# Two network layers on eight images: seven assisted taps and shift sums on ScalarE in image 0, an unfolded layernorm in image 1, large banks for the last gelus

## The chip, the cores and the metric

The kernel runs on one core of a Trainium2 chip. The metric is the device time of one execution in microseconds (us), the median of several runs. Engines are named PE (TensorE, the matrix engine), DVE (VectorE), ACT (ScalarE), POOL (GpSimd, which here issues DMAs only) and SP (SyncE, also DMAs only). Each engine takes its instructions in the order in which they were written for it; across engines, semaphores set the order.

## The reference, cut to what matters

The input is eight images of 384 channels on 32 x 32 points, all in float32. Layer 0 is a transformer block on the 1,024 points, layer 1 a convolution block:

```python
xn = layernorm(xf, g1, beta1)                       # first layernorm  (ln1)
q, k, v = split(xn @ w_qkv.T + b_qkv)               # 8 heads of 48
out = softmax(q @ k.T * SCALE) @ v
x1 = out @ w_proj.T + b_proj + shortcut
xn2 = layernorm(x1, g2, beta2)                      # second layernorm (ln2)
h = gelu(xn2 @ w_fc1.T + b_fc1)                     # 1536 wide
x = x1 + h @ w_fc2.T + b_fc2

y = conv_7x7_depthwise(x, dw_w) + dw_b
y = layernorm(y) * ln_w + ln_b                      # third layernorm  (ln3)
y = gelu(y @ w1 + b1)
gx = sqrt(sum over points of y*y);  nx = gx / (mean(gx) + eps)
y = grn_gamma * (y * nx) + grn_beta + y
return x + y @ w2 + b2
```

## The kernel before, in words

**Tiles.** Channels lie on the 128 partitions: an image is CT = 3 channel tiles of N = 1024 points, handled in halves of NH = 512. The hidden layer has HT = 12 tiles. The PSUM accumulators come from two pools: two large banks of 1024 columns (tag `s`, made by `s_tile`, used for attention's scores, for every second product of fc2 and for some sums) and four small ones of 512 columns (tag `o`, made by `o_tile`). A tile whose pool is exhausted waits until the last reader of the oldest one is done. A matmul of 128x512 in float32 is two records in the trace and takes U = 0.857 us.

**Order of the work.** The program is straight-line code. The matmuls are written out by hand, and each advances a planned clock (`flow.pe(us)`) of the class `Flow`. Work of the other engines is written as generators that are handed to `flow.spawn`; a generator emits its next instructions when the planned clock passes the wait that it yielded last. `flow.finish(chain)` emits all that a generator has left at once, at that place of every queue. So the planned waits decide where an instruction stands in its engine's queue, and nothing else; when it runs is up to the chip.

**Stages.** For image b the program writes: q and k, attention, the first half of fc1 (twelve tiles `fc1_b_0_m`, each followed by a gelu on ACT, L457 through `other_table`), the second half, fc2, and then layer 1 of image b-1: the w1 products (`grn_up`, whose matmuls are `h_*`), the values of the next image, and the w2 products. The depthwise convolution of image b-1 runs beside image b.

**The convolution.** It has 49 taps for each channel tile. DVE does most of them (`convolution`, L1102, about 1.15 us each). The generator `help_convolution` takes the last `helped` taps of each channel tile: ACT multiplies half an image by the tap (L1123, 128x512) into one of four buffers, and POOL issues a DMA of 256 KB that adds the result to the accumulator (L1124). HELPED is 7; image 0 has `HELPED + 2` (L1668). When fc1's first half of image b ends, `end_soon` finishes both generators, waits a planned time, and then the third layernorm of image b-1 runs (`conv_norm`).

**The third layernorm.** `abreast` runs two `layernorm` generators, one for each half. The sum over the channels is a matmul with a matrix of ones (`token_sums`). With a fold, a DMA by POOL first adds one half of the partitions to the other, and two 64-row matmuls that fill one after the other of the partition halves do the rest at half the price; with `fold=None` it is one 128x512 matmul of full price without a DMA. The first layernorm of image b+1 (`norm_of_next`) runs at about the same time and keeps its folds; its sums use the large banks, its variances the small ones. For these two norms DVE subtracts the mean (L1740 and L513), ACT squares, DVE adds the squares, and the variances go through ln and exp on ACT.

**fc2.** `by_thirds` forms fc2 of images 0 to 6 out of fifteen products of four matmuls, p0 to p14, alternately in a small and a large bank; DVE makes their operands and adds the products to `x` (L954 and L957). At the end `pad_half` copies `x` into the padded image with ACT (L891).

**Image 0's attention.** There the DVE also prepares weights, among them two shifts: the bias of w1 gets the layernorm's shift times w1 added (`shift_through_w1`), that of w2 the GRN's shift times w2 (`shift_through_w2`). Column sums on PE (L273, 128x1 each, into a large bank) give what is added; DVE adds the bias by L1501 (three columns at once, two groups for each of two steps) and L1519 (one column, three times). The scores of attention use the same large banks. The row sums of the softmax go through a chain for each pair of heads: ACT copies (L717), DVE adds (L719), a DMA carries out the row sums, DVE takes the reciprocal (L726), DMAs carry it back as `r`, and DVE multiplies (L745) before the projection.

**The last image.** `mlp_by_halves` does fc1 and fc2 one half of the points after the other. After fc2 of the first half, DVE adds (L895) and ACT pads (L891); twelve tiles of fc1's second half follow with their gelus. In the same stretch DVE does the last image's convolution and the third layernorm of image 6, whose sums lie in the large banks.

Of the kernel before, what the change touches and what calls it, by code (L numbers as in the profile page):

```python
# [46 lines left out]
F32 = mybir.dt.float32  # L47
# [4 lines left out]
P = 128  # L52
# [123 lines left out]
def block_kernel(  # L176
# [73 lines left out]
    def col(name, i):  # L250
        at, width = VEC[name]
        assert i < width
        return vec[:, at + i : at + i + 1]
# [7 lines left out]
    def o_tile(name):  # L261
        return ps_o.tile([P, NH], F32, tag="o", name=name)

    def weighted(dst, part, name, k):

        if k == 0:
            nc.vector.tensor_scalar(dst, part, col(name, 0), None, ALU.mult)
        else:
            nc.vector.scalar_tensor_tensor(dst, part, col(name, k), dst, ALU.mult, ALU.add)
# [6 lines left out]
    def columns(name):  # L276
        at, width = VEC[name]
        return vec[:, at : at + width]
# [93 lines left out]
            flow.pe(2 * U)  # L372
        return ps

    def linear_half(lhsT, rhs, nk, h, name):
        ps = o_tile(name)
        for k in range(nk):
            nc.tensor.matmul(out=ps, lhsT=lhsT(k), rhs=rhs(k)[:, half(h)], start=(k == 0), stop=(k == nk - 1))  # L378
            flow.pe(U)
        return ps  # L380
# [75 lines left out]
    def other_table(dst, src, function, **kw):  # L456
        nc.scalar.activation(dst, src, function, **kw)  # L457
        table[0] = None

    def s_tile(name):  # L460
        return ps_s.tile([P, N], F32, tag="s", name=name)

    def token_sums(t, name, fold, wait, bank):

# [408 lines left out]
                    nc.sync.dma_start(out=other, in_=own)  # L873
                proj("x", xt, qt * P // NH)

    def gelu_half(hid, m, h, xn, weights, wname, name):
        w = weights.at(wname, m // CM)[:, m % CM * CT : (m % CM + 1) * CT, :]
        ps = linear_half(lambda k: w[:, k, :], lambda k: xn[:, k, :], CT, h, f"{name}_{h}_{m}")
        other_table(hid[:, m, half(h)], ps, AF.Gelu, bias=bfc1[:, m : m + 1])

    def difference(dst, more, less):
# [150 lines left out]
    def mlp_by_halves(b, xt, xn, weights, ln, rest, between):  # L1032

        hid = one.tile([P, HT * N], F32, tag="big", name=f"hid_{b}").rearrange("p (m n) -> p m n", m=HT)
        for h in range(2):
            wa, wb = f"fc1_{b}_{h}", f"fc2_{b}_{h}"
            flow.finish(ln)
            for m in range(HT):
                gelu_half(hid, m, h, xn, weights, wa, f"fc1_{b}")
                if m % CM == CM - 1:  # L1040
                    weights.used(wa, m // CM)
                if m == 5 and h == 0:
                    rest()
                    ln = flow.spawn(layernorm(xt, xn, 1, eps0, "g2", f"ln2_{b}", True, slow=2.0))
                if m == HT - 1 and h == 0:
                    between(0, -1, ln)
            for ct in range(CT):
                keys = RAW[2 * ct : 2 * ct + 2]
                tiles = [weights.at(wb, key)[:, k, :] for key in keys for k in range(6)]
                ps = linear_half(lambda k: tiles[k], lambda k: hid[:, k, :], HT, h, f"fc2_{b}_{ct}_{h}")  # L1050
                for key in keys:
                    weights.used(wb, key)
                add_first(xt, ct, h, ps)
                pad_half(xt, ct, h)
                between(h, ct)
# [48 lines left out]
            n += 1  # L1104
            yield share * next((early for m, early in first if n <= m), us)

    def help_convolution(acc, us, taken, helped):

        yield 8.0
        for ct in reversed(range(CT)):  # L1110
            taken[ct] = float("inf")
            for i in TAPS[KS * KS - helped :]:
                dy, dx = divmod(i, KS)
                for h in range(2):
                    if quiet:
                        while quiet:
                            yield 1.0
                        yield 3.0
                    t = three.tile([P, NH], F32, tag="res", bufs=4, name=f"tap_{ct}_{i}_{h}")
                    y0 = dy + h * H // 2  # L1120
                    window = pad[:, ct, y0 : y0 + H // 2, dx : dx + W]
                    tap = col("dww", ct * KS * KS + i)
                    nc.scalar.mul(t.rearrange("p (h w) -> p h w", w=W), window, tap)  # L1123
                    nc.gpsimd.dma_start(out=acc[:, ct, half(h)], in_=t, accum_op=ALU.add)  # L1124
                    yield us
            taken[ct] = flow.now + 8.0
        yield 8.0
        taken.clear()
# [187 lines left out]
    def after(first, chain, us=0):  # L1316
        if us:
            yield us
        while first is not None and first.gi_frame is not None:
            yield 1.0  # L1320
        yield from chain
# [88 lines left out]
    def prepare(weights, aside):  # L1410
# [72 lines left out]
        def shift_through_w1():  # L1483
            for i in range(0, HT // 2, CT):
                t = one.tile([P, CT, N], F32, tag="xn", bufs=2, name=f"w1_lnb_{i}").rearrange("p c n -> p (c n)")
                t = t[:, : CT * 6 * P]
                nc.gpsimd.dma_start(out=t, in_=w1[:, i * 6 * P : (i + CT) * 6 * P])
                t = t.rearrange("p (i a o) -> p i a o", a=6, o=P)
                yield 22.0
                for r, order in enumerate(((0, 1, 2), (5, 3, 4))):  # L1490
                    dst = t[:, :, order[0], :]
                    nc.vector.tensor_scalar(dst, dst, col("lnb", 0), None, ALU.mult)
                    for k in (1, 2):
                        nc.vector.scalar_tensor_tensor(dst, t[:, :, order[k], :], col("lnb", k), dst, ALU.mult, ALU.add)
                yield 5.0
                ps = ps_s.tile([P, N], F32, tag="s", name=f"b1_{i}")
                for r, a in enumerate((0, 5)):
                    for k in range(CT):
                        column_sums(ps, r * CT + k, t[:, k, a, :])
                    m = i + r * HT // 2  # L1500
                    nc.vector.tensor_tensor(b1[:, m : m + CT], ps[:, r * CT : (r + 1) * CT], columns("b1")[:, m : m + CT], ALU.add)  # L1501

        def shift_through_w2():
            for r in range(CT):
                t = blocks(f"w2_gbeta_{r}")
                for s in range(2):
                    nc.gpsimd.dma_start(out=t[:, s], in_=chunk(w2, 2 * r + s).rearrange("p (k o) -> p k o", o=P))
                yield 14.0
                h = HT // 2
                for s in range(2):  # L1510
                    g = columns("gbeta")[:, s * h : (s + 1) * h].unsqueeze(2).to_broadcast((P, h, P))
                    nc.vector.tensor_tensor(t[:, s], t[:, s], g, ALU.mult)
                nc.vector.tensor_tensor(t[:, 0], t[:, 0], t[:, 1], ALU.add)
                for k in range(1, h):
                    nc.vector.tensor_tensor(t[:, 0, 0, :], t[:, 0, 0, :], t[:, 0, k, :], ALU.add)
                yield 8.0
                ps = ps_s.tile([P, N], F32, tag="s", name=f"b2_{r}")
                column_sums(ps, 0, t[:, 0, 0, :])
                nc.vector.tensor_tensor(b2[:, r : r + 1], ps[:, :1], col("b2", r), ALU.add)  # L1519

        if aside:
            yield from shift_through_w1()
# [92 lines left out]
    def main():  # L1615
# [49 lines left out]
        def start_conv(b, us, *first):  # L1665
            acc = state["acc"] = one.tile([P, CT, N], F32, tag="acc", name=f"acc_{b}")
            taken = {}
            helped = HELPED if b else HELPED + 2  # L1668
            state["conv"] = flow.spawn(convolution(acc, us, first, taken=taken, helped=helped), paced=True)
            state["help"] = flow.spawn(help_convolution(acc, 2.7, taken, helped), paced=True)  # L1670

        def conv_norm(b, ln):

            if b == 0:
                xn = state["xn"]
                norm = abreast(xn, xn, eps0, "g1", "ln1_1", True, gentle=True)
                state["norm1"] = flow.spawn(after(ln, norm))
            else:
                acc = state["acc"]
                how = dict(wait=5.0, late=3.5) if b < B - 1 else dict(factor=2.4, bank=s_tile)  # L1680
                norm = abreast(acc, acc, eps1, "lnw", f"ln3_{b - 1}", True, **how)
                if b < B - 1:
                    state["norm1"] = flow.spawn(after(ln, norm_of_next(b, 22.0 if b > 1 else 34.0)))
                    state["norm3"] = flow.spawn(after(ln, sequence(end_soon(b), norm)))
                else:
                    state["norm3"] = flow.spawn(after(ln, after(state["help"], after(state["conv"], norm))))
# [17 lines left out]

        def end_soon(b):
            end_convolution(b)
            yield 16.0 if b > 1 else 28.0

        def norm_of_next(b, us):

# [302 lines left out]
```

## Time and profile before

| quantity | value |
|---|---|
| median of 5 runs | 3269.34 us (3268.52 to 3273.7) |
| profiled execution | 3269.43 us, span 3267.7 us |
| granted TensorE clock, mean | 0.995 |
| PE busy | 3231.8 us (99%) |
| DVE busy | 2423.1 us (74%) |
| ACT busy | 1669.7 us (51%) |
| POOL busy | 486.9 us (15%) |

The busy time of an engine is the time in which it ran at least one instruction. A line of the timeline is a run of like instructions: its start and length in us, engine, source line, operation, output and inputs, shape, number, and in brackets the idle time of the engine ahead of it and what ended it. A line of the waits is engine, line, what it waited for, then the total in us, how often, and the longest. A line of the windows is start and end in us, length, then busy time with the number of instructions for PE, weight loads, DVE, ACT and POOL, the granted TensorE clock (1.00 is full), the mean busy share of the DMA engines and GB/s.

### The profile page before, as it was taken

What the parts mean: (1) busy time and instruction counts of PE and PEld (TensorE: products, weight loads), DVE (VectorE), ACT (ScalarE), POOL (GpSimd) and SP (SyncE); (2) the same over time, 40 slices, a digit from 0 to 9 for tenths busy, and PEclk for the clock granted to TensorE, in tenths of its full rate; (3) what the DMA queues carried; (4) which work ended last, traced back from release to release, by engine and by line L of the source; (5) the groups of instructions that cost most, each with busy time, mean ns of one, the idle gap of its engine ahead of it and who ended that gap; (6) DMA issues with size and microseconds to landing.
All of it is one profiled execution on the core that took longest, in us unless ns stands there. A gap on an engine that the chain in (4) does not pass through costs nothing. (4 is left out here: it accounts for less than half of the span.)

```text
span 3267.7 us, 38881 instructions
## 1 busy us (share of the span) xinstructions
PE 3231.8 (99%) x14204; PEld 1390.5 (43%) x14204; DVE 2423.1 (74%) x3309; ACT 1669.7 (51%) x2328; POOL 486.9 (15%) x575
## 2 busy tenths in 40 slices
PE   9999998999999999999999999999999999999999
PEld 5334433443344433444344443344434444344455
DVE  4544786778877878678787787876878778879940
ACT  3452664365743566434754537636475375723641
POOL 2111212102211121101212012110211102200000
PEclk9999999999999999999999999999999999999999
DMA  6535744638426473355734466353843638433231
GB/s 213 209 111 121 162 91 76 146 98 190 95 58 161 112 171 79 66 157 127 151 75 99 130 169 123 62 127 105 198 94 58 149 100 197 79 79 91 63 97 54
DMA packets 204114, 387.70 MB, mean 119 GB/s; under 512 B 41232, under 2 KB 46992, under 8 KB 203536
## 3 DMA queue, kind: packets, MB, share of 16 engines
q0 software_dynamic: 82880, 169.38, 27.6%
q1 hardware_dynamic: 120752, 215.09, 21.7%
q8 instruction: 114, 1.87, 0.2%
q10 hardware_dynamic: 288, 0.71, 0.1%
q14 instruction: 80, 0.66, 0.1%
HBM read 199.61 MB, written 38.14 MB: 73 GB/s over the span
## 5 line engine op out<-in xcount | busy, mean ns | idle before, releaser
L1102 DVE SCALAR_TENSOR_TENSOR acc<-pad,vec,acc 128x930 f32<-128x930 f32 (+8 forms) x855 | 956.2, 1154 | 29.1 <-DMA acc<-tap 24.3
L767 ACT ACTIVATE p<-s 128x1024 f32<-128x1024 f32 x512 | 524.4, 1025 | 275.3 <-PE s L758 268.9
L758 PE MATMUL s<-qk 48*64 48x512 f32 x4096 | 540.4, 594 | 6.1 <-DVE b_f L1519 5.6
L778 PE MATMUL o<-p,v 64*64 64x512 f32 x4096 | 537.0, 591 | 0.0
L378 PE MATMUL fc<-xn,fc 128*128 128x512 f32 x1152 | 506.2, 596 | 17.2 <-ACT hid L457 15.0
L1124 POOL DMA_DIRECT2D acc<-tap x306 | 263.9, 873 | 1449.3 <-ACT tap L1123 710.1
L378 PEld LDWEIGHTS fc<-xn,fc 128*128 128x128 f32 x1152 | 217.6, 190 | 301.6 <-issue 271.9
L445 PE MATMUL fc_p<-hid,fc 128*128 128x512 f32 x728 | 318.1, 593 | 1.1 <-DVE hid L957 0.6
L778 PEld LDWEIGHTS o<-p,v 64*64 64x64 f32 x4096 | 160.7, 133 | 282.9 <-issue 277.2
L758 PEld LDWEIGHTS s<-qk 48*64 48x64 f32 x4096 | 157.0, 133 | 289.2 <-issue 228.3
L457 ACT ACTIVATE hid<-fc,bfc_f 128x512 f32<-128x512 f32 x192 | 129.4, 684 | 286.8 <-PE fc L378 286.6
L445 PE MATMUL o_p<-y,w 128*128 128x512 f32 x624 | 270.9, 592 | 0.0
L1123 ACT ACTIVATE tap<-pad,vec 128x512 f32<-128x512 f32 x306 | 224.7, 735 | 19.0 <-DMA acc<-tap 19.0
L445 PEld LDWEIGHTS fc_p<-hid,fc 128*128 128x128 f32 x728 | 137.5, 190 | 178.4 <-issue 169.9
L445 PEld LDWEIGHTS o_p<-y,w 128*128 128x128 f32 x624 | 118.0, 190 | 148.7 <-issue 134.9
L1102 DVE SCALAR_TENSOR_TENSOR acc_last<-pad,vec,acc_last 128x377 f32<-128x377 f32 (+24 forms) x288 | 177.2, 688 | 0.6
L891 ACT COPY pad<-x 128x512 f32<-128x512 f32 x48 | 30.1, 634 | 254.4 <-DVE x L957 196.2
L719 DVE TENSOR_TENSOR attn<-o,attn 128x512 f32<-128x512 f32 x64 | 44.1, 689 | 131.3 <-ACT attn L717 131.3
L700 PE MATMUL proj<-attn,wproj_sb 128*128 128x512 f32 x288 | 127.2, 595 | 0.0
L678 PE MATMUL v<-wv_sb,xn 128*128 128x384 f32 x384 | 126.8, 487 | 0.0
L432 DVE TENSOR_TENSOR y<-h_n,y 128x512 f32<-128x512 f32 x72 | 49.8, 692 | 62.2 <-PE h_n L416 59.9
L678 PEld LDWEIGHTS v<-wv_sb,xn 128*128 128x128 f32 x384 | 72.5, 190 | 50.1 <-issue 3.4
(376 smaller groups left out, 4054.9 us busy)
## 6 DMA issues: line engine op xcount, KB each, us to landing
acc<-tap POOLq DMA_DIRECT2D x306, 256.0 KB, 3.5
fc<-s_fc SPq DMA_DIRECT2D x91, 256.0 KB, 4.0
w<-s_w SPq DMA_DIRECT2D x72, 320.0 KB, 3.5
hid<-hid POOLq DMA_DIRECT2D x42, 512.0 KB, 7.5
fc<-in_wfc SPq DMA_DIRECT2D x54, 384.0 KB, 4.1
w<-s_w SPq DMA_DIRECT2D x78, 256.0 KB, 2.7
y<-y POOLq DMA_DIRECT2D x36, 512.0 KB, 6.9
w_A<-in_w SPq DMA_DIRECT2D x36, 384.0 KB, 3.3
```

Of the source, the lines that this page charges most:

```text
L378: nc.tensor.matmul(out=ps, lhsT=lhsT(k), rhs=rhs(k)[:, half(h)], start=(k == 0), stop=(k == nk - 1))
L432: nc.vector.tensor_tensor(c[dst], banks(name), c[other], ALU.add)
L445: nc.tensor.matmul(out=bank, lhsT=lhsT, rhs=rhs, start=k == 0, stop=k == len(pairs) - 1)
L457: nc.scalar.activation(dst, src, function, **kw)
L678: nc.tensor.matmul(out=ps[:, :C], lhsT=xn[:, k, t * P : (t + 1) * P], rhs=wv_sb[:, k, :], start=(k == 0), stop=(k == CT - 1),)
L700: nc.tensor.matmul(out=ps, lhsT=wproj_sb[:, m, ct * P : (ct + 1) * P], rhs=attn[:, m, :], start=(m == 0), stop=(m == CT - 1),)
L758: nc.tensor.matmul(out=s[64 * i : 64 * i + 64, j, :], lhsT=kT[64 * j : 64 * j + HD, m, k0 : k0 + 64], rhs=qT[64 * j : 64 * j + HD, m, half ...
L767: nc.scalar.activation(p, s, AF.Exp)
L778: nc.tensor.matmul(out=outs[i][64 * j : 64 * j + 64, :], lhsT=v[keys, t, at : at + 64], rhs=p[keys, j, :], start=(t == 0), stop=(t == KT - 1),
L1102: nc.vector.scalar_tensor_tensor(dst, window, tap, dst, ALU.mult, ALU.add)
L1123: nc.scalar.mul(t.rearrange("p (h w) -> p h w", w=W), window, tap)
L1124: nc.gpsimd.dma_start(out=acc[:, ct, half(h)], in_=t, accum_op=ALU.add)
```

## The change

Four edits:

- Image 0 gets seven helped taps for each channel tile, as the others: twelve half taps fewer on ACT and POOL in all, six more taps on DVE.
- The fifteen shift sums of image 0 are read out of PSUM by ACT, one column an instruction (12 and 3 activations), in place of 4 and 3 adds on DVE.
- In image 1 the third layernorm of image 0 has no folds; its planned waits are stretched (`slow=1.6`), the wait ahead of it goes from 28 to 33, and that of the first layernorm of image 2 from 34 to 37.
- In the last image the gelus of fc1's second half read from the two large banks instead of the four small ones, and the sums of the third layernorm of image 6 lie in small banks.

The order of the other engines' instructions is the same from image 2 on; PE's own order differs only around the norms of image 1.

```diff
-    def linear_half(lhsT, rhs, nk, h, name):
-        ps = o_tile(name)
+    def linear_half(lhsT, rhs, nk, h, name, bank=o_tile):
+        ps = bank(name)[:, :NH]
...
-    def gelu_half(hid, m, h, xn, weights, wname, name):
+    def gelu_half(hid, m, h, xn, weights, wname, name, bank=o_tile):
...
-        ps = linear_half(lambda k: w[:, k, :], lambda k: xn[:, k, :], CT, h, f"{name}_{h}_{m}")
+        ps = linear_half(lambda k: w[:, k, :], lambda k: xn[:, k, :], CT, h, f"{name}_{h}_{m}", bank)
...
-                gelu_half(hid, m, h, xn, weights, wa, f"fc1_{b}")
+                gelu_half(hid, m, h, xn, weights, wa, f"fc1_{b}", s_tile if h else o_tile)
...
-            for i in TAPS[KS * KS - helped :]:
+            for i in TAPS[KS * KS - HELPED :]:
...
-                    nc.vector.tensor_tensor(b1[:, m : m + CT], ps[:, r * CT : (r + 1) * CT], columns("b1")[:, m : m + CT], ALU.add)
+                    for k in range(CT):
+                        bias = dict(bias=col("b1", m + k), scale=1.0)
+                        nc.scalar.activation(b1[:, m + k : m + k + 1], ps[:, r * CT + k : r * CT + k + 1], AF.Identity, **bias)
...
-                nc.vector.tensor_tensor(b2[:, r : r + 1], ps[:, :1], col("b2", r), ALU.add)
+                nc.scalar.activation(b2[:, r : r + 1], ps[:, :1], AF.Identity, bias=col("b2", r), scale=1.0)
...
-            helped = HELPED if b else HELPED + 2
-            state["conv"] = flow.spawn(convolution(acc, us, first, taken=taken, helped=helped), paced=True)
-            state["help"] = flow.spawn(help_convolution(acc, 2.7, taken, helped), paced=True)
+            state["conv"] = flow.spawn(convolution(acc, us, first, taken=taken, helped=HELPED), paced=True)
+            state["help"] = flow.spawn(help_convolution(acc, 2.7, taken), paced=True)
...
-                how = dict(wait=5.0, late=3.5) if b < B - 1 else dict(factor=2.4, bank=s_tile)
+                how = dict(wait=5.0, late=3.5, fold=b > 1, slow=1.0 if b > 1 else 1.6) if b < B - 1 else dict(factor=2.4)
...
-                    state["norm1"] = flow.spawn(after(ln, norm_of_next(b, 22.0 if b > 1 else 34.0)))
+                    state["norm1"] = flow.spawn(after(ln, norm_of_next(b, 22.0 if b > 1 else 37.0)))
...
-            yield 16.0 if b > 1 else 28.0
+            yield 16.0 if b > 1 else 33.0
```

## The prediction

> **What bounds the kernel now.** First the page's busy times:
>
> ```profile
> PE 3231.8 (99%) x14204; PEld 1390.5 (43%) x14204; DVE 2423.1 (74%) x3309; ACT 1669.7 (51%) x2328; POOL 486.9 (15%) x575
> ```
>
> TensorE is the bound; an edit pays only where it moves PE. Next the chain of waits of PE, all of it over 1.7 us:
>
> ```profile
> PE fc L378 <- ACT hid L457: 15.0, 1, 15.0
> PE s L758 <- DVE b_f L1519: 5.6, 1, 5.6
> PE fc L378 <- DVE x L895: 2.2, 1, 2.2
> PE h_n L416 <- ACT y L437: 1.8, 1, 1.8
> ```
>
> The change touches the places of all four. Third, the timelines around them: the 5.6 us (PE, then DVE), the 15.0 us (ACT, DVE), the 2.2 us (PE, DVE, ACT).
>
> ```profile
> 127.09 1.98 PE L758 MATMUL s<-qk 48*64 48x512 f32 x8 [5.57 <-DVE b_f L1519]
> ```
> ```profile
> 126.89 0.15 DVE L1519 TENSOR_TENSOR b_f<-b,vec 128x1 f32<-128x1 f32 x1
> ```
> ```profile
> 536.68 0.74 ACT L1123 ACTIVATE tap<-pad,vec 128x512 f32<-128x512 f32 x1 [2.70 <-DMA acc<-tap]
> ...
> 554.89 0.74 ACT L1123 ACTIVATE tap<-pad,vec 128x512 f32<-128x512 f32 x1 [2.04 <-DMA acc<-tap]
> 555.54 2.40 ACT L457 ACTIVATE hid<-fc,bfc_f 128x512 f32<-128x512 f32 x4
> ```
> ```profile
> 559.26 12.85 DVE L1102 SCALAR_TENSOR_TENSOR acc<-pad,vec,acc 128x899 f32<-128x899 f32 x11 [22.62 <-DMA acc<-tap]
> ```
> ```profile
> 2943.39 7.89 PE L378 MATMUL fc<-xn,fc 128*128 128x512 f32 x18
> 2953.44 10.66 PE L378 MATMUL fc<-xn,fc 128*128 128x512 f32 x24 [2.16 <-DVE x L895]
> ```
> ```profile
> 2952.64 0.74 DVE L895 SCALAR_TENSOR_TENSOR x<-fc,vec,x 128x512 f32<-128x512 f32 x1
> ```
> ```profile
> 2953.41 0.63 ACT L891 COPY pad<-x 128x512 f32<-128x512 f32 x1 [2.98 <-DVE x L895]
> 2954.07 1.28 ACT L457 ACT_TABLE_LOAD   x1
> 2955.36 2.42 ACT L457 ACTIVATE hid<-fc,bfc_f 128x512 f32<-128x512 f32 x4
> ```
>
> Last the clock by windows: PE shows 0.50 in 127.10–132.90 (after the 5.57 us wait) and in 556.20–559.60 (after the 15.0). After the waits of 2.16 and 1.75 it shows 1.00.
>
> ```profile
> 127.10:132.90 5.80, 5.80 (x28) 1.78 (x32) 2.47 (x8) 1.31 (x2) 1.08 (x2) 0.50 0.98 356
> 556.20:559.60 3.40, 3.34 (x4) 1.52 (x5) 0.34 (x1) 1.75 (x4) 0.57 (x1) 0.50 0.44 77
> 2953.40:2980.00 26.60, 26.56 (x67) 11.36 (x68) 25.85 (x50) 14.82 (x20) 1.61 (x2) 1.00 0.32 74
> ```
>
> Half a clock costs about half the stretch: 2.9 us after the first wait, 1.9 after the second (its 60 records took 27.62 us, 60 undisturbed ones 25.72).
>
> **Image 0's attention: ScalarE reads the sums.** PE stood for 5.57 us because the one-column add of L1519 is queued on DVE behind gapless work from 114.02 on. ScalarE has no such queue there: its exponentials (1.02 us) come every 1.72. The wait and its 2.9 us of half clock go: up to 8.5. Against that: 15 small reads on ScalarE, none shown in the trace; nearest row is a 128x12 activation of 0.21 us, a 128x512 copy takes 0.58 (bounds 0.15, DVE's time for the same add, and 0.58). At 0.21 three reads take 0.63, so each of the two waits of 0.25 between two sum groups (102.11 and 141.56) grows by 0.5: −1.0. The six reads also push ScalarE's copy of 101.30 back by up to 2.9 us (it then falls behind an exponential), which delays the first row-sum chain (reciprocal, DMA out and back) by 1 to 1.8. Next late is that chain's end: `r` came back at 140.52 while DVE multiplied at 142.70; now that multiply can run at 140.52 + 1.4 = 141.9, 0.8 earlier. The projection needs the chain's last product (155.67) only after two matmuls of 0.857, so it can start at 155.67 − 1.71 − 0.8 = 153.2 instead of 156.78: 3.6; with a delay of 1, 4.0. I take **−3.8**, bounds −2.5 and −6.5 (8.5 less 1.0 and 1.0 of w_lnb's wait, if the chain holds nothing).
>
> **Image 1: seven taps, no folds.** Nine helped taps per channel tile were not through when fc1's first half ended, so the rest was emitted at once, ahead of the gelus; each pair waits for accumulating DMAs (4.4 us a pair). Twelve tap halves fewer at 2.2 us each are 26 us, more than the 18.2 from 536.68 to 554.89: the last tap now comes before that point and the gelus follow their matmuls. That frees 15.01 + 1.90 = 16.9 us. DVE gets six more taps (6 × 1.15 = 6.9 us), and does the 21 taps left from 536.6 to 561 and four adds to 564: 7.5 us ahead of its first later use, so they cost nothing.
>
> But the same DVE work now meets an earlier PE. I walked the new order with the rows' pitches (tile of fc1 2.57; a four-matmul product of fc2 3.43; three subtractions 1.84; adds 0.60 to 0.72; 1024-wide adds 1.13). The order after: fc1 ends at 566.8; fc2's second product waits for a large bank that DVE frees at 573.2 (three subtractions): 2.0. The third norm's sums, now 2 × 0.857 on PE without a DMA, fit; its variances wait for squares added on DVE: 1.3 and 0.5. The first norm's variances still take a folding DMA (add done 594.9, landing in 2.7 to 3.6): 2.1. Products end at 629.7; DVE ends its adds at 633.4, where its row stood at 644.94, and the padding copies behind it let the next matmul start 1.2 later, 634.6 instead of 646.13. So 11.5 of 16.9 come home; DVE had idled only 7.1 us from 585.0 to 644.94, so it is next late. **−11.5**, bounds −9 (a fold landing in 8.4, as 512 KB transfers do, partly hidden) and −14 (DVE's idle filled).
>
> **Last image: two banks for the gelus.** Before, PE ran three tiles (18 records, two a matmul, 7.89 us) ahead of the gelus, then waited 2.16 for a bank that DVE freed at L895. ScalarE's own queue is the longer one: the padding copy waits for that same L895, then 0.63 of copy and 1.28 of table load, and gelus start at 2955.36. No cause of these moves, as DVE is busy without a gap from 2908. With two large banks PE does two tiles, to 2948.5, and the third needs the first gelu done, at about 2956.1: it waits 7.6 instead of 2.16 and stands one tile less far: 2956.1 − 2953.44 + 2.57 = +5.2. It also meets the table loads of the layernorm later with one tile less ahead: +0.6. And the wait is as long as those that halved the clock: rows say 1.9 and 2.9, I take 2.5 (bounds 0, as after the 2.16, and 3.4). **+8.3**, bounds +5 and +9.5.
>
> The Trainium skill ("TensorE: Matmul & The Clock Gate", Part 1: The HAM clock gate) says that TensorE falls to half rate after one idle window of about 3.4 us and returns after a busy one of the same length. As an estimate from that rule alone, the 7.6 us wait halves the clock for 3.4 us and costs 1.7, the sum −7.8; the row of 5.80 us at 0.50 says that it can last longer, and the rows decide. The rule speaks against this part.
>
> The third norm's sums move to small banks: no wait found, nothing.
>
> **Sum.** −3.8 − 11.5 + 8.3 = −7.0 us. The profiled execution took 3269.43 us (span 3267.7), the median is 3269.34: 3262.4. About 0.2% (6.5 us) is what a measurement can tell from no change, so the forecast lies at that line.
>
> **Rivals.**
> A. The DVE chains hold less than walked: part one −6.5, image 1 −14, last image +5.2 (no half clock): −15.3, 3254.1. For it: ScalarE and DVE idle around both waits. Against: DVE's 7.1 us of idle in 60, and the two clock rows.
> B. New short waits add up: the four in image 1 (2.0, 1.3, 0.5, 2.1) within 31 us bring the clock down once (1.9) and image 0 gives only 2.5: −7.0 + 1.9 + 1.3 = −3.8, 3265.6. Against: 1.00 after 2.16 and 1.75.
> C. Slower. The helper's chain still ends late: DVE waits for the last accumulating DMA as it did until 559.26, the 22.62 us row. With six more taps it then has 17 × 1.155 = 19.6 and four adds of 0.68, to 581.6 instead of 564, 10.2 beyond the 7.5 of slack. Everything behind it is 10.2 later, and PE's wait halves the clock (2.9): −7.0 + 13.1 = +6.1. It passes +6.5 if that DMA lands after 559.7; at 561, 3277. For it: the taps run at 2.2 us each by DMA, not by plan. Against: 12 fewer of them are worth 26 us.
>
> **How the numbers follow.** Forecast 0.55 (0.32 beyond the line, 0.23 within it), A 0.18, B 0.17, C 0.10. Faster 0.50, same 0.40, slower 0.10. The range leaves out C and half of A: 3255 to 3269; the forecast's own is 3259 to 3267.
>
> **What would show it.** Right: no PE wait of 5 us or more in image 0's attention, the projection near 153; no tap among the gelus after 536; PE waits on DVE of 1 to 2.5 us between 570 and 635, `h_n` resuming near 631 in the new clock (3.8 us earlier); in the last image a PE wait of 7 to 8 us on ACT hid L457 with 0.50 after it. Wrong: a DVE wait on acc<-tap of 10 us or more in image 1; a fold that PE waits over 5 us for; no long wait in the last image, which would take +8.3 away and make it 3254.

## The result and the profile after

The changed kernel takes 3272.26 us (median of 24 runs; before 3270.62 in 44 runs beside it): a ratio of 1.0008, 95% interval 1.0002 to 1.0014. That is within 0.2% of no change, 2.6 us to the slow side, where 7 us to the fast side had been forecast and 3255 to 3269 was the range. Its profiled execution took 3278.05 us (span 3276.2), 6 us over its median; a second profiled execution (the fifth run below) took 3271.20. Parts are therefore given as means over the executions that share them; each kernel has one profiled execution, the changed one two.

The page's busy times, then the chain of waits of PE:

```profile
PE 3241.1 (99%) x14196; PEld 1396.5 (43%) x14196; DVE 2429.3 (74%) x3308; ACT 1664.4 (51%) x2331; POOL 473.3 (14%) x559
```
```profile
PE fc L381 <- ACT hid L460: 7.7, 2, 7.4
PE proj L700 <- DVE attn L745: 4.7, 2, 4.0
PE s L758 <- ACT qk L604: 4.3, 3, 2.6
PE h_n L419 <- ACT y L440: 2.1, 1, 2.1
PE fc_p L448 <- DVE xn L1741: 2.1, 1, 2.1
PE ln_var L1726 <- DMA ln<-ln: 1.4, 1, 1.4
PE b L276 <- ACT b_f L1503: 1.3, 2, 0.7
```

The waits of 15.0 and 5.6 us are gone, and most waits foretold are there at their forecast size: 7.4 in the last image (forecast 7.6), 2.1 on the subtractions (2.0), 0.74 and 1.35 on the first norm's variances (2.1 together), 2.1 at `h_n`. Those on the third norm's variances are shorter, 0.22 and 0.27 (1.3 and 0.5). What was not foretold is PE's busy time: 3241.1 us, 9.3 more than before, for eight records fewer. About half of it is the clock: from 80 us on PE was busy at half clock for 23.1 us, before for 12.7, and half of the 10.4 us more, 5.2, is what that costs. The windows show four of the places. Columns: start and end, length, busy PE, weight loads, DVE, ACT, POOL, granted clock, DMA share, GB/s.

```profile
101.90:105.30 3.40, 2.75 (x28) 1.76 (x24) 0.00 (x0) 1.99 (x7) 2.65 (x5) 1.00 0.63 198
105.30:108.70 3.40, 3.40 (x24) 1.04 (x20) 0.69 (x1) 1.62 (x3) 0.00 (x0) 0.50 1.00 395
```
```profile
153.10:156.50 3.40, 0.35 (x1) 0.30 (x2) 1.29 (x5) 0.00 (x0) 0.54 (x1) 1.00 0.90 222
156.50:159.90 3.40, 3.40 (x5) 1.35 (x4) 2.84 (x10) 0.00 (x0) 0.00 (x0) 0.50 0.89 315
```
```profile
596.80:600.20 3.40, 1.39 (x6) 0.45 (x8) 0.00 (x0) 1.94 (x4) 1.88 (x2) 1.00 0.91 181
600.20:607.10 6.90, 6.90 (x11) 2.51 (x8) 0.02 (x1) 1.32 (x2) 0.00 (x0) 0.51 0.69 121
```
```profile
2948.60:2955.40 6.80, 0.16 (x1) 0.00 (x0) 6.10 (x13) 3.81 (x6) 0.00 (x0) 0.75 0.21 58
2955.40:2958.80 3.40, 2.62 (x3) 1.17 (x4) 3.33 (x7) 1.29 (x3) 0.23 (x1) 0.50 0.00 0
2958.80:2962.20 3.40, 3.40 (x5) 1.33 (x4) 3.40 (x8) 0.50 (x1) 1.38 (x2) 0.50 0.50 77
```

Each fence starts with a stretch in which PE lacked work and goes on with what ran at half clock behind it. The last one follows the long wait that the forecast had priced; there the clock fell within the wait. The others follow 0.66 us between two groups of column sums, 3.98 us ahead of the projection, and 0.74 plus 1.35 us in fc2.

Set against before, place by place (starts of the same PE instructions; means over the executions of this and the following kernels that have the place unchanged, their number in brackets; the kernel before is one execution, 1.2 us under its median):

| place | forecast | measured, mean | single executions |
|---|---|---|---|
| image 0, first shift sum to the second half's projection | -3.8 | -1.2 (8) | -3.2 to +0.8 |
| from there to image 1's fc1 (waits at that projection) | 0 | +0.7 (9) | 0.0 to +2.2 |
| image 1, start of fc1 to the first score of image 2 | -11.5 | -6.1 (5) | -6.9 to -5.2 |
| images 2 to 6 | 0 | +1.6 (9) | -0.4 to +6.9 |
| last image, from fc1's second half on | +8.3 | +8.1 (5) | +7.1 to +8.7 |

The sum is +3.1; the ratio says 2.6. Image 0 is counted from 101 us because the clock between 65 and 78 us, ahead of all that the change touches, moves its start by up to 4 us from one execution to the next.

### The profile page after: what moved, and what is told of

Its sections match the earlier page's. It is cut to its first block, busy times and chain, and to the rows that moved or that the text cites. A ratio compares the mean times of both kernels' runs of the same rounds, so it can differ in the third digit from the quotient of the medians.

```text
span 3276.2 us, 38832 instructions
## 1 busy us (share of the span) xinstructions
PE 3241.1 (99%) x14196; PEld 1396.5 (43%) x14196; DVE 2429.3 (74%) x3308; ACT 1664.4 (51%) x2331; POOL 473.3 (14%) x559
## 5 line engine op out<-in xcount | busy, mean ns | idle before, releaser
L1102 DVE SCALAR_TENSOR_TENSOR acc<-pad,vec,acc 128x870 f32<-128x870 f32 (+8 forms) x861 | 962.9, 1154 | 6.8 <-DMA acc<-tap 1.7
L1124 POOL DMA_DIRECT2D acc<-tap x294 | 252.8, 872 | 1439.8 <-ACT tap L1123 714.8
L1123 ACT ACTIVATE tap<-pad,vec 128x512 f32<-128x512 f32 x294 | 215.9, 735 | 9.8 <-DMA acc<-tap 9.8
```

The lines of the kernel that those rows point to most:

```text
L1102: nc.vector.scalar_tensor_tensor(dst, window, tap, dst, ALU.mult, ALU.add)
```

## The experiments

All ratios are to the kernel before on the same chip, with 95% intervals.

**1. The fourth part undone.**

```diff
-                gelu_half(..., f"fc1_{b}", s_tile if h else o_tile)
+                gelu_half(..., f"fc1_{b}")
-  else dict(factor=2.4)
+  else dict(factor=2.4, bank=s_tile)
```

> The changed kernel with its fourth part undone: the gelus of fc1's second half read the four small banks again, and the sums of the third layernorm of image 6 lie in large ones. Theory (the places add up: the last image costs 8.5 us, image 1 gives 7.4, image 0 under 1): the wait of 7.4 us on ACT L460 becomes one of 2.2 on DVE x, with a clock of 1.00 after it; 8.5 us less than the changed kernel, a ratio to before of about 0.998. Rival (the time is lost in images 2 to 6, where the changed kernel's profile has new waits of 2.55, 1.60 and 0.95 us on ACT behind helped taps, with half clock after the first): those waits are there again, and the ratio stays between 0.9995 and 1.0005.

3264.66 us, 0.9983 (0.9975 to 0.9992): the theory's number, and the rival's range is excluded. The 7.4 us wait is 2.21 again. Images 2 to 6 cost 0.9 us, so the 6.9 in the changed kernel's first profile was mostly of that execution. The clock did not stay at 1.00, though: after the 2.21 us wait one stretch ran at 0.5, which the waits of 2.16 and 1.75 us had not done in the profile before; the last image costs 1.5 us by it. The wait of 2.07 us in image 1 shows the same lottery. First the changed kernel's windows around it, then this one's:

```profile
569.50:572.90 3.40, 2.43 (x12) 0.55 (x10) 0.94 (x2) 0.80 (x2) 0.00 (x0) 1.00 0.26 75
572.90:576.30 3.40, 2.30 (x6) 1.14 (x7) 1.26 (x3) 1.05 (x2) 0.00 (x0) 1.00 0.04 15
576.30:579.80 3.50, 3.50 (x10) 1.59 (x9) 3.50 (x7) 0.00 (x0) 0.00 (x0) 1.00 0.00 0
```
```profile
572.40:575.90 3.50, 1.43 (x10) 0.51 (x10) 1.89 (x3) 1.84 (x3) 0.00 (x0) 0.99 0.27 75
575.90:579.30 3.40, 3.40 (x5) 1.35 (x4) 0.12 (x1) 0.00 (x0) 0.00 (x0) 0.51 0.00 0
```

The wait is the same. The granted clock changes only at the borders of a fixed grid of 3.413 us (worked out below). There the wait is split between two stretches of the grid, 2.43 and 2.30 us busy, and the clock stays; here it lies in one, 1.43 us busy, and the next runs at half.

**2. Two large banks for two gelus.**

```diff
-                gelu_half(..., f"fc1_{b}", s_tile if h else o_tile)
+                gelu_half(..., f"fc1_{b}", s_tile if h and m < 2 else o_tile)
```

> The changed kernel, but only the first two gelus of fc1's second half in the last image read large banks, the other ten small ones. Theory (PE waits because only two banks are free while ScalarE's queue stands behind the padding copy and the table load until 2956): two tiles in large banks and three in small ones are 12.9 us of matmuls from 2943.4, as long as that queue takes, so the wait falls from 7.4 to under 1 us, the clock stays at 1.00 and the time is 10 us below the changed kernel's, a ratio of about 0.9977. Rival (the small banks are not free either, held by the sums of the third layernorm that moved there or by fc2 until DVE has read them at about 2953): PE still waits 2 to 5 us, and the ratio is 0.9985 to 1.000.

3265.91 us, 0.9983 (0.9974 to 0.9992). The timeline of PE:

```profile
2935.25 18.19 PE L381 MATMUL fc<-xn,fc 128*128 128x512 f32 x42
2955.39 1.08 PE L484 MATMUL ln_var<-ln_sq,ones 64*64 64x512 f32 x4 [1.96 <-DMA ln_sq<-ln_sq]
```

Seven tiles run without a wait, so it was the number of banks. But PE then arrives at the layernorm's variances 1.96 us before their folding DMA has landed: the 2.2 us of before have moved, not gone. The last image costs +0.1 against before. The interval holds the theory's 0.9977 and the rival's 0.9985 alike; the timeline, not the time, decides against the rival's reason, as no small bank was waited for.

**3. The variances later.**

```diff
-            yield 8.0
+            yield 8.0 if b > 1 else 14.5
             sums = [total(square, h, "var") for h, _, square in pairs]
```

> The changed kernel, but in image 1 the planned wait ahead of the first layernorm's variances is 14.5 instead of 8, which puts their four small matmuls behind fc2's eighth product instead of inside the seventh. Theory (PE waits 0.74 and 1.35 us there for the folding DMA, and this brings the half clock of 600 to 607): both waits go, the windows from 600 to 607 show 1.00, and image 1 ends 2.1 + 3.4 = 5.5 us sooner, unless DVE is late with its adds to x at the end, then 2 to 3 us; ratio 0.999. Rival (the half clock comes from the many short matmuls and short waits from 574 on, not from these two): the waits go, 0.5 stays somewhere between 590 and 615, and the gain is 2 us or less.

3263.57 us, 0.9978 (0.9969 to 0.9987). Both waits and the half clock of 600 to 607 are gone, `h_n` waits 1.0 us, and image 1 gives 13.1 us in place of 6.1. The gain is larger than the theory's 5.5; what the rest of it is was not traced.

**4. The multiply behind the add, image 0.**

```diff
-        yield 2.4 if hurry else 5.0
+        yield 2.4 if hurry else 11.0 if (b, qh, m) == (0, 0, 1) else 5.0
         nc.vector.tensor_tensor(attn[:, m, :], attn[:, m, :], r, ALU.mult)
```

> The changed kernel, but in image 0 the planned wait ahead of the multiply L745 of the third pair of heads of the first half is 11 instead of 5, which puts that multiply behind the add L719 of the last pair, for which the projection waits. Theory (DVE stood 6.98 us at this multiply for a DMA, and the add behind it in DVE's queue started the last chain 4.4 us late): the projection's wait of 3.98 us goes to under 0.5 with the half clock after it, 4 to 6 us less than the changed kernel, ratio 0.9993. Rival (the last chain is held by its own DMAs, out, back and broadcast on SP's queue): the add moves to 138.5, but the last multiply stays near 155 and PE still waits over 3 us; ratio 1.0005 or more.

3264.13 us, 0.9979 (0.9971 to 0.9988). DVE's timeline, first of the changed kernel, then of this one:

```profile
142.22 0.69 DVE L745 TENSOR_TENSOR attn<-attn,r 128x512 f32<-128x512 f32 x1 [6.98 <-DMA r<-back]
142.83 0.68 DVE L719 TENSOR_TENSOR attn<-o,attn 128x512 f32<-128x512 f32 x1
...
155.41 0.69 DVE L745 TENSOR_TENSOR attn<-attn,r 128x512 f32<-128x512 f32 x1 [2.08 <-DMA r<-back]
```
```profile
138.13 0.69 DVE L719 TENSOR_TENSOR attn<-o,attn 128x512 f32<-128x512 f32 x1 [2.15 <-ACT attn L717]
...
149.66 0.69 DVE L745 TENSOR_TENSOR attn<-attn,r 128x512 f32<-128x512 f32 x1 [0.35 <-DMA r<-back]
```

The last chain's add moves from 142.83 to 138.13, its multiply from 155.41 to 149.66, and the projection waits for nothing. Image 0 gives 8.6 us in place of 1.2. So the chain through DVE's queue was the limit, not the DMAs.

**5. The changed kernel again.** No edit.

> The changed kernel itself once more, beside the three below. Theory (what its profile shows between images 2 and 6, 7.2 us of waits behind helped taps with a half clock, is chance of one execution): those waits are mostly absent, under 2 us, and its places repeat: image 0 -1 to -2, image 1 -5 to -7, last image +8.5 to +9 against before; the ratio is again 1.0005 to 1.001. Rival (the change brings them about): they come again within 2 us of the same size.

3271.14 us, 1.0003 (0.9994 to 1.0012). Image 0 +0.8, image 1 -6.7, images 2 to 6 +2.3, last image +7.6. The waits behind helped taps come again with 1.6 and 0.8 us at two of the former places, but the one of 2.55 us with its half clock does not. Image 1 is as expected, image 0 and the last image lie outside what was expected of them, and one wait of 1.6 us came again at its full size: the theory held in part.

**6. The waits filled with matmuls.**

```diff
+  if kind == "var" and b == 1:            # ahead of each variance sum: 1 and 2 matmuls
+      for _ in range(1 + h):
+          nc.tensor.matmul(out=ps[:, :C], lhsT=ones, rhs=wv_sb[:, 0, :], start=True, stop=True)
...
+  if h and m == 2:                        # last image, ahead of the third tile: 11
+      spare = o_tile("filler")
+      for _ in range(11):
+          nc.tensor.matmul(out=spare[:, :C], lhsT=ones, rhs=wv_sb[:, 0, :], start=True, stop=True)
```

> The changed kernel with extra matmuls of 128x384 (0.64 us each, results unused) queued on PE in two of its waits: one and two ahead of the two variance sums of the first layernorm in image 1, eleven ahead of the third tile of fc1's second half in the last image. Every wait for another engine stays as long as it is. Theory (the clock is halved for a stretch of 3.41 us when PE was busy for less than about 0.43 of the stretch of 3.41 us before): 1.00 from 597 to 607 and from 2949 to 2962, image 1 3.4 us shorter and the last image 2.6, 6 us less than the changed kernel. Rival (the clock falls because of the wait's own length or of what stands behind it): 0.50 shows at the same places and the time is the changed kernel's or up to 2 us more.

3265.06 us, 0.9990 (0.9981 to 0.9999), 6.1 us below the changed kernel beside it. The windows:

```profile
593.80:597.20 3.40, 3.34 (x12) 1.12 (x12) 0.00 (x0) 1.99 (x4) 1.92 (x2) 1.00 0.94 178
597.20:600.60 3.40, 3.40 (x10) 1.25 (x8) 0.00 (x0) 1.32 (x2) 0.00 (x0) 1.00 1.12 194
```
```profile
2942.20:2945.60 3.40, 3.05 (x9) 1.34 (x8) 3.37 (x8) 1.95 (x3) 0.00 (x0) 1.00 0.00 0
2945.60:2949.00 3.40, 3.40 (x10) 1.49 (x9) 3.37 (x7) 0.69 (x1) 1.61 (x2) 1.00 0.43 65
```

PE does nothing useful in the waits, no other engine is quicker, and image 1 gives 10.1 us in place of 6.1 and the last image costs 5.6 in place of 8.1: that is the half clock alone. It is caused by PE's idleness, not by what is waited for.

**7. The taps alone.** The kernel before with HELPED taps for image 0.

```diff
-            helped = HELPED if b else HELPED + 2
+            helped = HELPED
```

> The kernel before with the first part alone: seven helped taps for image 0, nothing else. Theory (the taps alone end the wait of 15.0 us, and the third layernorm without folds only spares PE short waits for DMAs): no wait over 3 us in image 1, its end 4 to 10 us sooner; ratio 0.997 to 0.999. Rival (the folds' DMAs queue on POOL and the earlier PE meets them): PE waits 5 us or more in the norms' sums or variances, and most of the gain is gone, ratio over 0.999.

3253.32 us, 0.9951 (0.9937 to 0.9965). Image 1 gives 16.5 us, all that the 15.0 us wait and its half clock held, and the largest wait left in it is 1.7 at `h_n`. That is more than the theory's 4 to 10 us, and this one line does more than the whole change. PE's timeline at the first layernorm's sums, of this kernel and then of the changed one:

```profile
565.62 1.09 PE L1724 MATMUL ln_sum<-ln,ones 64*64 64x512 f32 x8
566.64 5.42 PE L448 MATMUL fc_p<-hid,fc 128*128 128x512 f32 x12
```
```profile
567.32 3.60 PE L448 MATMUL fc_p<-hid,fc 128*128 128x512 f32 x8
570.84 1.09 PE L1726 MATMUL ln_sum<-ln,ones 64*64 64x512 f32 x8
574.00 1.10 PE L448 MATMUL fc_p<-hid,fc 128*128 128x512 f32 x2 [2.07 <-DVE xn L1741]
```

With the planned wait of 34 the sums stand ahead of fc2's first product, and DVE has freed the large bank by the time the second product needs it. With 37 they stand behind it, and the second product waits. That the later subtractions then make the later squares, folds and waits is read from the order of the queues; the 37 was not tried alone.

**8. The three moves together.** The changed kernel with the edits of 2, 3 and 4.

> The changed kernel with the three edits of the second to fourth run together: two large banks only for the first two gelus, the first layernorm's variances in image 1 later, and the multiply behind the last pair's add in image 0. Theory (the three places are independent): image 0 gives 8 us against before, image 1 11 to 13, the last image 0 to 1; 20 us less than before, ratio 0.994. Rival (what is won early is spent later in waits on DVE or on DMAs, as PE runs ahead): under 14 us, ratio over 0.9957.

3250.96 us, 0.9941 (0.9927 to 0.9955), 19 us less than before: image 0 -6.3 (one stretch at half clock behind the column sums, 1.7), image 1 -13.1, last image +1.7 (half clock after the fold's 1.98 us). Between image 0's place and image 1's a new wait of 2.14 us at the second half's projection takes 2.2 back.

**9. Folds kept, new planned waits.**

```diff
-  dict(wait=5.0, late=3.5, fold=b > 1, slow=1.0 if b > 1 else 1.6)
+  dict(wait=5.0, late=3.5, slow=1.0 if b > 1 else 1.6)
```

> The changed kernel with the folds of the third layernorm in image 1 kept; its new planned waits (1.6, 33 and 37) stay. Theory (what eats most of the taps' 16.5 us in image 1 is where the planned waits put the two norms: the variances of image 2's first norm inside fc2's seventh product, and its subtractions ahead of a large bank): the wait of 2.07 us and a wait for those variances come again, with half clock in some windows, and image 1 gives 5 to 9 us; ratio 1.000 to 1.001. Rival (the four 128x512 matmuls without folds are the cost): image 1 gives 14 us or more, ratio under 0.9985.

3276.60 us, 1.0018 (1.0009 to 1.0028). Image 1 gives 4.4 us, less than with the folds taken out. PE's timeline:

```profile
570.40 5.37 PE L448 MATMUL fc_p<-hid,fc 128*128 128x512 f32 x8 [2.07 <-DVE xn L1741]
...
594.69 2.70 PE L1726 MATMUL ln_var<-ln,ones 64*64 64x512 f32 x8 [2.25 <-DMA ln<-ln]
```

The waits come at the same places: the new planned waits are what costs, and the missing folds do not. Under these planned waits they seem to save about 2 us, by one execution with folds against five without. The time was higher than expected, and image 1 gave less than the 5 to 9 us expected; the waits are the expected ones. A kernel without folds under the old planned waits was not tried.

**10. The reads alone.** The kernel before with the two reads by ScalarE.

> The kernel before with the second part alone: ScalarE reads the shift sums. Theory (of the 8.5 us of wait and half clock most comes back as the projection's wait of 4 us for the multiply of the last pair and a half clock behind it): from the first sums at 101 to the projections' end 1 to 2 us are won, all else as before, ratio 0.9994 to 0.9999. Rival (the reads alone would give the forecast 3.8 us, and the fewer taps or another part disturbed them): ratio 0.9988 or less.

3272.92 us, 1.0008 (0.9999 to 1.0017). The 5.6 us wait is gone; the projection waits 3.81 us, with half clock behind it, and two stretches from 100.6 and one from 134.7 run at half clock too. From the first sums to the second half's projection it is +0.6 us. Neither expectation held: the reads by themselves give nothing.

**11 and 12. What the runs point to.** Seven taps, the reads, the edit of 4, the third layernorm as before; and for 11 the edit of 2, for 12 the last image as before.

> Seven taps in image 0, ScalarE's reads, the multiply moved behind the last pair's add, the first two gelus of the last image in large banks, the third layernorm of image 1 as before. Theory (the places add up): image 0 gives 4 to 7 us, image 1 16.5, the last image 0 to -2; 20 to 23 us, ratio 0.9930 to 0.9940, below the taps alone. Rival (the projection's wait in image 0 comes back in another place): no more than the taps alone, 0.995.

> As the run before, but the last image's gelus and the sums of the third layernorm of image 6 lie where the kernel before has them. Theory: the wait of 2.2 us there costs as much as the wait for a folding DMA that the two large banks leave, so that the two runs differ by under 2 us; ratio 0.9930 to 0.9940. Rival (two large banks are worth the 2 us): 2 us slower than the run before.

3247.38 us, 0.9931 (0.9917 to 0.9944), and 3248.86 us, 0.9939 (0.9925 to 0.9953). They have the lowest medians of this study, but their intervals overlap with each other's and with those of runs 7 and 8. Image 0 gives 9.1 and 8.6 us (4 to 7 were expected), image 1 15.0 and 15.6 (16.5). The first one's largest waits of PE:

```profile
PE fc_p L448 <- DMA hid<-hid: 2.1, 1, 2.1
PE h_n L419 <- ACT y L440: 1.8, 1, 1.8
```

## Why the prediction was wrong

**The waits were right.** The tap chain ended in time, DVE did its 21 taps in one run and never waited for an accumulating DMA (rival C), and the waits that matter came at their places and sizes.

**The last image was right:** +8.1 against +8.3, by two tiles ahead instead of three, the wait of 7.4 and 2.6 us of half clock.

**The step that failed** is the last one of the reading, "After the waits of 2.16 and 1.75 it shows 1.00". From these two waits, which happened to keep the clock, it was taken that only waits of 5 us and more cost clock, and every wait that the change adds in images 0 and 1 was entered at its bare length. Another row of the same profile spoke against it and was left out. After a wait of 0.25 us between two groups of column sums it shows half clock, too:

```profile
141.56 0.83 PE L273 MATMUL b<-ones,w_lnb 128*128 128x1 f32 x6 [0.25 <-DVE b_f L1501]
```
```profile
143.20:146.60 3.40, 3.40 (x20) 1.04 (x16) 3.37 (x5) 1.02 (x1) 0.00 (x0) 0.51 0.03 4
```

In the runs all half-clock stretches inside the span are whole multiples of 3.413 us, the distance of a fixed grid. PE's busy share was worked out from the records for each full-clock stretch of that grid, over all 14 executions, from 80 us on. Below 0.40, all 25 were followed by half clock; between 0.40 and 0.65, 10 of 43; between 0.65 and 0.93, 14 of 147; above, none. All 14 lie in image 0's attention and hold 11 or 12 one-column sums; of 15 such stretches only one was not followed by half clock. So a wait of 2 us costs 1.7 more or nothing, by where it falls on the grid: the 2.07 us in image 1 were followed by half clock in five of the nine profiles that have them. The 0.74 + 1.35 us with short matmuls between cost 3.4 in three profiles and 1.7 in two.

The Trainium skill ("TensorE: Matmul & The Clock Gate", Part 1: The HAM clock gate) also states a free-running window of about 3.4 us; the 3.413 agrees. Its rule that idle gaps above about 3.4 us are to be avoided is too mild here: a gap of 2.07 us, with 1.43 us of work in 3.5, was enough. The forecast quoted the rule against the last image only; the 3.98 us ahead of image 0's projection are such a gap, too.

**Image 1, -6.1 in place of -11.5.** In the changed kernel's profile 3.4 of the 4.6 us that it misses are the half clock of 600 to 607. Run 6, where matmuls fill the waits and the clock stays at 1.00, gives 10.1 us in its one execution; so 4.0 of the mean's 5.4 are the clock, and the other 1.4 lie in the walk of the new order, where they were not traced. The 16.9 us ceiling was sound, as the taps alone give 16.5. The forecast let 5.4 of them go to the new order of the norms; it was 10.4.

**Image 0, -1.2 in place of -3.8.** The chain was sized well: the projection's third matmul starts 3.8 us sooner, counted from the first shift sum (158.49 - 101.03 against 156.15 - 102.51). But PE had to stand 3.98 us for it, and the stretch behind ran at half clock, 1.7. That wait is in the forecast's own sum: 8.5 less 1.0 less 3.8 leaves 3.7 us, entered without any clock. The column sums, whose wait grew from 0.25 to 0.66, were followed by no half-clock stretch in run 6 and by three in run 5, 1.7 us each, where the profile before has one. The forecast had put the growth at 0.5 and its clock at nothing.

**Rival B** named the mechanism (short waits bring the clock down) with too small a price, one stretch for 1.9; its evidence against was the same two waits. What the waits in images 2 to 6 depend on stays open. One of 1.26 to 1.60 us at the first score of image 5 is in eight of the 14 profiles, not in those of before, of the taps alone and of runs 2 and 9 to 11; one of 2.55 us at the first score of image 3 came once.

## What to carry to other kernels

Price a wait of PE by its length and by the share of PE's work left in the clock's stretch around it: two us in 3.4 may cost another 1.7, and the trace of one execution shows only where the grid fell that time. Read every stretch at half clock in the trace, also those behind short waits. When a change has several parts, cost each one against the best of the others alone: one line gave 16.5 us here, and the part beside it took 10 back. In queues served in order, ask which planned wait puts a waiting instruction ahead of the one that the end depends on; moving one multiply behind one add was worth 7 us.

## What the runs showed of the hardware that was not expected

The granted clock went by a stretch's share of work more than by the length of a wait: all 25 stretches under 0.40 busy were followed by half clock, and the same 2.07 us wait was followed by it in five profiles of nine. Column sums of 128x1 seem to count little: a stretch of 2.75 us busy in 3.40 (0.81), with twelve of them, was followed by 0.50. Idle matmuls in a wait pay: 14 of them, whose results nothing reads, took 6.1 us off the time.
